# Two attentions with the context on the partitions: maximum and sum by GpSimd, and a written order of the steps

## The chip, the cores and the metric

The kernel runs on one core of a Trainium2 chip. The core has five instruction streams that matter here: TensorE (PE, with its weight loads shown as PEld), VectorE (DVE), ScalarE (ACT), GpSimd (POOL), and SyncE (SP), which in this kernel issues the DMAs. Each engine takes its instructions strictly in its own order and waits where an operand is not ready. The metric is device microseconds of one execution, and less is better.

## The reference

A stack of four layers works on `x` (8 sequences x 112 tokens x 512 channels) with a context of 8 x 375 x 512, all in float32. The first layer is a one-head attention, the second and third are RWKV blocks, the fourth has two 16-head cross attentions and an MLP. The change concerns the two 16-head attentions of the fourth layer:

```python
def _cross_attention(q_in, kv_in, wq, bq, wk, bk, wv, bv, wo, bo, bias_k, bias_v):
    qh = (q_in @ wq + bq).reshape(b, q_len, H, K)          # H = 16 heads of K = 128
    kh = (kv_in @ wk + bk).reshape(b, t, H, K)             # t = 375 context tokens
    vh = (kv_in @ wv + bv).reshape(b, t, H, K)
    kh = concatenate([kh, broadcast_to(bias_k, (b, 1, H, K))], axis=1)   # token 376
    vh = concatenate([vh, broadcast_to(bias_v, (b, 1, H, K))], axis=1)
    logits = einsum('bqhk,bthk->bhqt', qh, kh) / sqrt(K)
    weights = softmax(logits, axis=-1)                     # over the 376 tokens
    ctx = einsum('bhqt,bthk->bqhk', weights, vh).reshape(b, q_len, H * K)
    return ctx @ wo + bo

x = x + _cross_attention(layer_norm1(x), context, ...)
x = x + _cross_attention(layer_norm2(x), context, ...)
x = x + gelu(layer_norm3(x) @ w_fc1 + b_fc1) @ w_fc2 + b_fc2
```

## The kernel before

Everything is held with channels on the 128 partitions: `x` as 4 blocks of 128 channels by 896 tokens (8 batches of 112). The 16 heads are worked in `NG` = 4 groups of `HG` = 4. The value projections of both attentions and part of the first one's keys are made long before, as filler under the RWKV layers, and lie in DRAM (`wvs`, `wks`). The other keys are made inside the attentions, for two batches at a time, by seven block products instead of eight (`chained`, line L1234 for the matmuls, L1237 to L1243 for the copies and adds); one call has 14 pieces. Query and output projections are also seven block products (`seven` and `project7`, L1161; 14 pieces). The sums of weight blocks that these need come from `weight_sums`, four GpSimd operations on 128x512 each (L1135 to L1138), the sums of tokens from `token_sums` on DVE (L1143 to L1146).

For each attention, `attention` loops over the groups, and in each over the 8 batches. For one batch of one group:

- the keys' last column, `bias_k - bk`, is copied by POOL (L1396); the values of the batch are loaded by two DMAs (L1398, L1399) into one buffer;
- for each of the 4 heads one matmul gives the scores, 112 query tokens on the partitions by 376 context tokens (L1403); `softmax` takes the maximum along the free axis on DVE (L232), the exponential with its running sum on ACT (L235), reciprocal and product on DVE (L236, L237); three transposes on TensorE (L1406) turn the result, so that context tokens lie on the partitions;
- the three transposed chunks of 125, 125 and 126 tokens are copied from PSUM (L1410 on ACT, L1412 on DVE), 12 matmuls give the weighted values (L1416), and DVE adds the value bias (L1423).

Then the group's output projection and the next group's queries follow, interleaved. In this stage no order is written out: the framework's scheduler orders the instructions of every engine by its own priorities, and the kernel influences it only through the order in which Python makes them and through the `fill` calls, which put key pieces between the steps of the layer norms. Stages before this one (first layer, RWKV) have `manual_schedule` regions, in which the instructions of PE, DVE, ACT and POOL stand as the program writes them. DMAs on SP are not bound by such a region.

PSUM has eight banks: two for products (`mm`), two for scores, three for transposes, one for weighted values.

Of the kernel before, what the change touches and what calls it, by code (L numbers as in the profile page):

```python
# [29 lines left out]
P = 128  # L30
# [11 lines left out]
HG = 4  # L42
NG = HEADS // HG
T = S + 1
CT = S // 3
# [63 lines left out]
def tile_kernel(ctx: ExitStack, tc: tile.TileContext, d: dict, out: bass.AP):  # L109
# [27 lines left out]
    ones_t, mean_h, less_mean_h = (const.tile([P, P], F32, name=f) for f in ("ones_t", "mean_h", "less_mean_h"))  # L137
    pick = const.tile([P, 4, 4 * HB], F32, name="pick")
# [89 lines left out]

    def softmax(work, scores, n, name):

        top = work.tile([L, 1], F32, tag="top", name=f"top_{name}")
        nc.vector.tensor_reduce(top, scores, AX.X, ALU.max, negate=True)  # L232
        prob = work.tile([L, n], F32, tag="prob", name=f"prob_{name}")
        total = work.tile([L, 1], F32, tag="total", name=f"total_{name}")
        nc.scalar.activation(prob, scores, AF.Exp, bias=top, accum_out=total)  # L235
        nc.vector.reciprocal(total, total)  # L236
        nc.vector.tensor_scalar(prob, prob, total, None, ALU.mult)  # L237
        return prob
# [883 lines left out]
    def weight_sums(pool, tag, w, u):  # L1122


        if tag == "kt":
            y = [pool.tile([P, HG, T], F32, tag=tag, name=f"ws{j}{u}", bufs=4) for j in range(2)]
# [8 lines left out]
        nc.gpsimd.tensor_add(y[0], a21, a22)  # L1135
        nc.gpsimd.tensor_sub(y[1], y[0], a11)
        nc.gpsimd.tensor_sub(y[2], a11, a21)
        nc.gpsimd.tensor_sub(y[3], a12, y[1])  # L1138
# [9 lines left out]
    def seven(ps, work, w, s, b, t, n, put, u):  # L1148
# [25 lines left out]
        for m in range(2):  # L1174
            first.append(bank("k1", m))
            product(first[m], m, lambda k: w[:, k], b11)
            yield
            p1.append(tile_of("rstd", m))
            nc.scalar.copy(p1[m], first[m])
        for m in range(2):  # L1180
            product(first[m], m, lambda k: w[:, 2 + k], b21, start=False)
            yield
            put(0, m, first[m], None)
        for m in range(2):
            p = bank("k6", m)
            product(p, m, lambda k: s()[1][:, k], t[1])
            yield
            u2 = tile_of("u2", m)
            nc.vector.tensor_add(u2, p, p1[m])
            p = bank("k7", m)  # L1190
            product(p, m, lambda k: s()[2][:, k], t[2])
            yield
            u3 = tile_of("u3", m)
            nc.vector.tensor_add(u3, p, u2)
            q = bank("k5", m)
            product(q, m, lambda k: s()[0][:, k], t[0])
            yield
            put(1, 2 + m, q, u3)
# [68 lines left out]
    def attention(i, ident, h_in, work, kv, ps, ps2, keep, near, mlp_norm):  # L1267
# [104 lines left out]
        def some(pieces, n):  # L1372
            for _ in range(n):
                next(pieces)
# [249 lines left out]
```

## Time and profile before

| | us |
|---|---|
| median of 3 runs | 2945.32 (2944.32 to 2945.58) |
| span of the profiled execution, first to last instruction | 2938.3 |
| first key product of the fourth layer starts at | 1414.6 |
| first score matmul of the first 16-head attention at | 1471.9 |
| first score matmul of the second one at | 2126.1 |
| last weighted values end at about | 2742 |

The profiled execution's own time outside its span isn't listed; the median of the runs stands 7.0 us above the span, and this is taken as what lies around it. Times in a profile's row are the mean of one instruction unless said otherwise. An idle time is put beside the instruction that ended it, with what released it. A line of the chain of waits gives start, length and the instruction; a line of the table by stretch gives each engine's busy time in that stretch. TensorE's matmuls overlap, so the distance from one to the next, which the chain shows, is a better price than a row's mean.

### The profile page before, as it was taken

What the parts mean: (1) busy time and instruction counts of PE and PEld (TensorE: products, weight loads), DVE (VectorE), ACT (ScalarE), POOL (GpSimd) and SP (SyncE); (2) the same over time, 40 slices, a digit from 0 to 9 for tenths busy, and PEclk for the clock granted to TensorE, in tenths of its full rate; (3) what the DMA queues carried; (4) which work ended last, traced back from release to release, by engine and by line L of the source; (5) the groups of instructions that cost most, each with busy time, mean ns of one, the idle gap of its engine ahead of it and who ended that gap; (6) DMA issues with size and microseconds to landing.
All of it is one profiled execution on the core that took longest, in us unless ns stands there. A gap on an engine that the chain in (4) does not pass through costs nothing.

```text
span 2938.3 us, 29915 instructions
## 1 busy us (share of the span) xinstructions
PE 2848.3 (97%) x10130; PEld 1555.3 (53%) x10130; DVE 1605.4 (55%) x2408; ACT 1020.6 (35%) x2028; POOL 870.8 (30%) x700
## 2 busy tenths in 40 slices
PE   8989999999999999999899999999999999999999
PEld 4734443344444433356465656566565656656544
DVE  1464288845442788652555555545554554545455
ACT  2232456533243565532331313232331323323311
POOL 1432178744331687641412010100302010000030
PEclk9999999999999999999999999999999999999999
DMA  5721498843311989642243334334332433432110
GB/s 208 231 76 39 156 278 258 265 128 110 99 64 62 281 234 298 184 132 90 101 149 126 124 123 129 109 122 140 102 123 100 133 108 122 139 113 80 47 51 25
DMA packets 198743, 400.82 MB, mean 136 GB/s; under 512 B 33224, under 2 KB 119528, under 8 KB 191808
## 3 DMA queue, kind: packets, MB, share of 16 engines
q1 hardware_dynamic: 198592, 398.91, 43.2%
q8 instruction: 81, 1.33, 0.2%
q14 instruction: 70, 0.57, 0.1%
HBM read 321.06 MB, written 77.91 MB: 136 GB/s over the span
## 4 chain that ended last, share of the span: by engine, by line
PE 83%; DVE 9%; ACT 3%; POOL 3%; issue 2%; DMA 1%; DVEq 0%; POOLq 0%; ACTq 0%; SPq 0%
PE ps_vk L1001 13%; PE ps_k1k L1234 10%; PE ps_k5k L1234 7%; PE av L1416 6%; PE sc L1403 5%; PE ps_o L163 3%; PE pt L1406 3%; PE ps_fk L163 2%; PE ps_k1q L1161 2%; PE ps_r L569 2%; PE ps_k L569 2%; PE ps_k5q L1161 2%; PE ps_fr L163 2%; PE ps_v L569 2%; PE ps_k7q L1161 2%
## 5 line engine op out<-in xcount | busy, mean ns | idle before, releaser
L1001 PE MATMUL ps_vk<-wv,cv 128*128 128x512 f32 x1296 | 581.7, 599 | 13.8 <-ACT k L1099 6.1
L1001 PEld LDWEIGHTS ps_vk<-wv,cv 128*128 128x128 f32 x1296 | 242.8, 191 | 337.3 <-issue 285.0
L1027 POOL TENSOR_TENSOR k<-k,k 128x512 f32<-128x512 f32 (+1 forms) x153 | 197.2, 1289 | 323.4 <-ACT k L1026 276.0
L776 DVE TENSOR_TENSOR_SCAN st<-decay,kv 128x904 f32<-128x904 f32 x128 | 260.7, 2037 | 17.5 <-POOL rs L780 4.8
L780 POOL TENSOR_TENSOR rs<-st,r 128x896 f32<-128x896 f32 x128 | 246.8, 1928 | 51.9 <-DVE st L776 46.8
L235 ACT ACTIVATE prob<-sc,top 112x376 f32<-112x376 f32 x256 | 147.2, 575 | 296.3 <-DVE top L232 168.0
L1396 POOL COPY k<-over_k 128x4 f32<-128x4 f32 x64 | 13.8, 223 | 648.6 <-PE sc L1403 576.6
L1403 PE MATMUL sc<-k,q 128*112 128x376 f32 x512 | 201.2, 485 | 1.6 <-ACT prob L235 1.5
L1416 PEld LDWEIGHTS av<-pts,v 125*128 125x128 f32 (+1 forms) x1536 | 183.4, 191 | 31.0 <-DVE pts L1412 15.8
L1416 PE MATMUL av<-pts,v 125*128 125x112 f32 (+1 forms) x1536 | 187.7, 276 | 1.9 <-DVE pts L1412 0.9
L1234 PE MATMUL ps_k1k<-cs,wsk 128*128 128x375 f32 x480 | 177.8, 478 | 4.6 <-ACT u2k L1237 3.1
L772 DVE TENSOR_TENSOR kv<-vp,k 128x904 f32<-128x904 f32 x128 | 141.5, 1105 | 58.2 <-ACT vp L674 52.4
L232 DVE TENSOR_REDUCE top<-sc 112x1 f32<-112x376 f32 x256 | 139.0, 544 | 53.7 <-PE sc L1403 49.0
L1026 ACT COPY k<-ps_vk 128x512 f32<-128x512 f32 (+1 forms) x153 | 89.1, 582 | 177.0 <-PE ps_vk L1001 174.2
L1099 ACT COPY k<-ps_vk 128x512 f32<-128x512 f32 (+1 forms) x153 | 89.0, 582 | 172.3 <-PE ps_vk L1001 164.2
L1406 PEld LDWEIGHTS pt<-ident_l,prob 112*125 112x125 f32 (+1 forms) x768 | 97.3, 175 | 72.2 <-DVE prob L237 44.8
L1406 PE MATMUL pt<-ident_l,prob 112*125 112x112 f32 (+1 forms) x768 | 120.7, 276 | 2.7 <-DVE prob L237 2.5
L1234 PEld LDWEIGHTS ps_k1k<-cs,wsk 128*128 128x128 f32 x480 | 88.7, 188 | 62.8 <-ACT u2k L1237 4.3
L237 DVE TENSOR_SCALAR prob<-prob,total 112x376 f32<-112x376 f32 x256 | 113.4, 443 | 7.7
L1241 DVE TENSOR_TENSOR k<-ps_k5k,u2k 128x375 f32<-128x375 f32 x52 | 28.5, 549 | 162.2 <-PE ps_k5k L1234 161.2
L674 ACT COPY vp<-vj 128x896 f32<-128x896 f32 x124 | 112.8, 910 | 7.3 <-DMA vj<-rows 3.5
L1423 DVE TENSOR_TENSOR ctxt<-av,bv 128x448 f32<-128x448 f32 x64 | 40.0, 625 | 128.9 <-PE av L1416 128.9
(394 smaller groups left out, 4837.0 us busy)
## 6 DMA issues: line engine op xcount, KB each, us to landing
vj<-rows SPq DMA_DIRECT2D x124, 448.0 KB
cv<-blocks SPq DMA_DIRECT2D x181, 251.5 KB
cs<-blocks SPq DMA_DIRECT2D x120, 375.0 KB
wvs<-k SPq DMA_DIRECT2D x128, 256.0 KB
v<-wvs SPq DMA_DIRECT2D x64, 512.0 KB
cx<-in_ctxT SPq DMA_DIRECT2D x38, 750.0 KB
v<-wvs SPq DMA_DIRECT2D x64, 252.0 KB
wvs<-k SPq DMA_DIRECT2D x64, 224.0 KB
```

Of the source, the lines that this page charges most:

```text
L163: nc.tensor.matmul(p, w[:, k, o * P : (o + 1) * P], rhs(k, h), start=k == 0, stop=k == NC - 1)
L235: nc.scalar.activation(prob, scores, AF.Exp, bias=top, accum_out=total)
L569: nc.tensor.matmul(y, ws[f][:, c, o * P : (o + 1) * P], x_f, start=c == 0, stop=c == NC - 1)
L776: nc.vector.tensor_tensor_scan(flat(st), flat(decay[:, c]), flat(kv), 0.0, ALU.mult, ALU.add)
L780: nc.gpsimd.tensor_mul(by_batch(rs), st[:, :, :L], by_batch(r[:, c, :]))
L1001: nc.tensor.matmul(to, left, right, start=start and n == 0, stop=k == 1, skip_group_check=True)
L1027: nc.gpsimd.tensor_add(y, z, y)
L1161: nc.tensor.matmul(to, lhsT, rhs, start=start and k == 0, stop=k == 1, skip_group_check=not start)
L1234: nc.tensor.matmul(y, lhsT, rhs, start=start and k == 0, stop=k == 1, skip_group_check=True)
L1403: nc.tensor.matmul(sc, q[:, o, tok], kt[:, o, :], start=True, stop=True)
L1406: nc.tensor.transpose(pt[t][:nt, o, :], prob[:, t0 : t0 + nt], ident[:L, :L])
L1416: nc.tensor.matmul(av[:, o, :], v[:nt, t, o * HD : (o + 1) * HD], pts[:nt, t, o, :], start=t == 0, stop=t == 2,)
```

## The change

In the 16-head attentions, the scores are computed the other way round: keys are the stationary operand in three chunks of 128 context tokens (the chunks overlap by three; the keys' tiles have two more columns, `TK` = 378, for the last one), and the result has context tokens on the partitions and query tokens along the free axis. The transposes and their copies go away. The work is cut into units of two heads of one batch, 16 a group, 128 in all. For one unit (lines of the new file):

- `scores`: 6 matmuls of 112 columns (L1424); ACT copies the first chunk and DVE takes the maximum with the other two (L1432, L1434); GpSimd takes the maximum across the partitions and writes it to all of them (L1436, a `partition_all_reduce` of 128x224);
- `exponentials`: DVE subtracts the maximum from the three chunks, 672 columns (L1442); ACT takes the exponentials of 448 and 224 columns, with a bias of -1e30 on the rows that a chunk has too many (L1444);
- `chunk_sums`: two DVE adds of 224 columns (L1449, L1450); `total`: GpSimd sums across the partitions (L1454); `inverse`: DVE reciprocal of 128x224 (L1458);
- `weighted`: 6 matmuls (L1465) on the unnormalized exponentials; `finish`: DVE multiplies by the reciprocal (L1478), ACT adds the value bias (L1480).

The whole loop stands in a `manual_schedule` region. In step k the program writes: load of the values for unit k+1, sum across partitions of unit k-1, scores and maximum of unit k, reciprocal of k-1, a key piece, exponentials of k, a key piece, weighted values and finish of k-1, chunk sums of k, further key pieces. A count spreads the pieces of the next two batches' keys over four steps; where few are left, the last four steps take pieces of the output projection instead.

GpSimd does no additions in this stage any more: the weight sums, and the adds of `chained` outside the first norm, go to DVE. Values are loaded by half batches into three buffers. In `seven` and `chained` the evacuation of a product now stands before the generator's `yield` and not after it. PSUM has three banks for products, four for scores (two tiles of two), one for weighted values. Two constant tiles of the RWKV layers are freed before the fourth layer. The built program has two POOL instructions more that change the engine's loaded code, one ahead of the first maximum, one ahead of the MLP's weight sums.

```diff
-                for o in range(HG):
-                    sc = ps2.tile([L, T], F32, tag="sc", name=f"sc{u}_{o}", bufs=2)
-                    nc.tensor.matmul(sc, q[:, o, tok], kt[:, o, :], start=True, stop=True)
-                    prob = softmax(work, sc, T, f"{u}_{o}")
-                    for t, (t0, nt) in enumerate(CHUNKS):
-                        nc.tensor.transpose(pt[t][:nt, o, :], prob[:, t0 : t0 + nt], ident[:L, :L])
...
-                for t, (_, nt) in enumerate(CHUNKS):
-                    if t == 1:
-                        nc.scalar.copy(pts[:nt, t], pt[t][:nt])
-                    else:
-                        nc.vector.tensor_copy(pts[:nt, t], pt[t][:nt])
...
+        def scores(gr, k, q):
...
+            sc = ps2.tile([P, 4, 256], F32, tag="sc", name=f"sc{u}", bufs=2)
+            for t in range(3):
+                for y in range(2):
+                    o = 2 * half + y
+                    nc.tensor.matmul(
+                        sc[:, t, y * L : (y + 1) * L],
+                        kt[:, o, t * CT : t * CT + P],
+                        q[:, o, b * L : (b + 1) * L],
+                        start=True,
+                        stop=True,
+                    )
+            top = work.tile([P, n], F32, tag="top", name=f"top{u}", bufs=2)
+            nc.scalar.copy(top, sc[:, 0, :n])
+            for t in (1, 2):
+                nc.vector.tensor_max(top, sc[:, t, :n], top)
+            tops = work.tile([P, n], F32, tag="tops", name=f"tops{u}", bufs=1)
+            nc.gpsimd.partition_all_reduce(tops, top, P, ReduceOp.max)
+            return [u, gr, k, sc, top, tops]
+
+        def exponentials(it):
+            u, gr, k, sc, top, tops = it
+            pts = work.tile([P, 3, n], F32, tag="pts", name=f"pts{u}", bufs=2)
+            nc.vector.tensor_sub(pts, sc[:, :3, :n], tops.unsqueeze(1).to_broadcast([P, 3, n]))
+            for t, y in ((slice(2), 0), (slice(2, 3), 1)):
+                nc.scalar.activation(pts[:, t], pts[:, t], AF.Exp, bias=rests[:, y : y + 1])
+            it[3] = pts
+
+        def chunk_sums(it):
+            u, gr, k, pts, top, tops = it
+            nc.vector.tensor_add(top, pts[:, 0], pts[:, 1])
+            nc.vector.tensor_add(top, pts[:, 2], top)
+
+        def total(it):
+            each = work.tile([P, n], F32, tag="each", name=f"each{it[0]}", bufs=1)
+            nc.gpsimd.partition_all_reduce(each, it[4], P, ReduceOp.add)
+            it[5] = each
+
+        def inverse(it):
+            nc.vector.reciprocal(it[5], it[5])
...
+        with tc.manual_schedule(engines=ORDERED):
+            for gr in range(NG):
...
+                for k in range(2 * B):
+                    key = (i, gr, 2 * (k // 4) + 2) if k < 12 else (*following, 0) if following else None
+                    left = ready[key] - shared["emitted"] if key else 0
+                    if k == 12:
+                        early = left < 8 or following != (i, gr + 1)
+                        w_q = query_weight(gr + 1) if gr + 1 < NG else None
+                    count = left if early else -(-left // (4 - k % 4))
...
+                    if k + 1 < 2 * B:
+                        vs[k + 1] = load_values(gr, k + 1)
+                    if before:
+                        total(before)
+                    it = scores(gr, k, q)
+                    if before:
+                        inverse(before)
+                    take(more_keys(key, int(count > 1)))
+                    exponentials(it)
+                    take(more_keys(key, 1))
+                    if before:
+                        weighted(before, vs.pop(k - 1))
+                        finish(before, ctxt, t_c)
+                    chunk_sums(it)
+                    take(more_keys(key, count - 1 - int(count > 1)))
+                    if k == 1 and not ends:
+                        s_o = weight_sums(keep, "ws", w_o, f"o{i}_{gr}", nc.vector)
+                    if k >= 12 and early:
+                        take(out_pieces, 1)
+                    before = it
...
-            tc.tile_pool(name="t3p", bufs=2, space=PSUM) as ps,
+            tc.tile_pool(name="t3p", bufs=3, space=PSUM) as ps,
```

## The prediction

> **What bounds the kernel now.** I read the page's busy shares first, then the same shares by stretch, then the chain that ended last inside one head group, and last the groups with their durations. The page, engines with share of the span:
>
> ```profile
> PE 2848.3 (97%) x10130; PEld 1555.3 (53%) x10130; DVE 1605.4 (55%) x2408; ACT 1020.6 (35%) x2028; POOL 870.8 (30%) x700
> PEclk9999999999999999999999999999999999999999
> ```
>
> TensorE is busy 97% at an ungated clock; but a share is no limit, so the stretch of one head group (stretch, its length, busy time of PE, PEld, DVE, ACT, POOL, clock, DMA share, GB/s):
>
> ```profile
> 1872.00:2040.00 168.00, 167.66 (x691) 105.27 (x690) 84.27 (x191) 47.24 (x123) 17.14 (x20) 1.00 0.38 121
> ```
>
> PE has no hole in it, DVE is half idle, POOL nine tenths idle: in the attentions the time is PE's instructions, and these can be priced by the chain (start, length, what, records):
>
> ```profile
> 1913.78 1.26 PE ps_k5k L1234 x4
> 1930.20 1.26 PE sc L1403 x4
> 1933.35 0.66 PE pt L1406 x6
> 1939.18 2.67 PE av L1416 x24
> ```
>
> An f32 matmul is two records, a transpose one. So a score matmul of 376 columns costs 0.63 us, a transpose 0.11, a matmul of 112 columns 0.222, a key product of 375 columns 0.63.
>
> **Part 1: what leaves PE.** Removed are 256 score matmuls x 0.632 = 162 us and 768 transposes x 0.110 = 84 us; added 768 score matmuls of 112 columns (6 per unit of two heads of one batch, 128 units) x 0.222 = 171 us, by the row of `av`, which has that shape. The 768 matmuls of `av` stay. Net: 75 us less PE work. From the first key product at 1414.6 to the end, all PE work priced this way is 1467 of 1524 us; I take the other 57 us (norms, the MLP's starts) as unchanged. If PE stays the only limit, the span goes from 2938.3 to 2863.
>
> **Part 2: what the units now wait for.** The unit's chain in the new order is: POOL maximum (L1436), DVE subtraction from PSUM (L1442), ACT exponentials of 448 and 224 columns (L1444), DVE adds of the three chunks (L1449, L1450), POOL sum (L1454). On POOL's queue the sum of unit k stands ahead of the maximum of unit k+1, so the units do not overlap on this chain: it is a loop, and one turn is the shortest possible step. Rows for its links (line, engine, form, count, then busy, mean ns of one, idle before):
>
> ```profile
> L1423 DVE TENSOR_TENSOR ctxt<-av,bv 128x448 f32<-128x448 f32 x64 | 40.0, 625 | 128.9 <-PE av L1416 128.9
> L1241 DVE TENSOR_TENSOR k<-ps_k5k,u2k 128x375 f32<-128x375 f32 x52 | 28.5, 549 | 162.2 <-PE ps_k5k L1234 161.2
> L591 ACT ACTIVATE decay<-e 128x448 f32<-128x448 f32 x16 | 9.0, 576 | 0.3
> L1237 ACT COPY u2k<-ps_k1k 128x375 f32<-128x375 f32 x60 | 28.2, 471 | 47.7 <-PE ps_k1k L1234 47.7
> L1144 DVE TENSOR_TENSOR t_c<-ctxt,t_c 128x224 f32<-128x224 f32 x28 | 10.9, 389 | 0.5
> L706 DVE RECIPROCAL gsq<-gsq 128x224 f32<-128x224 f32 x32 | 48.2, 1523 | 24.7 <-ACT gsq L701 24.7
> ```
>
> Subtraction, 672 columns: DVE's PSUM rows rise 76 ns over 73 columns, so 625 + 224 x 1.04 = 0.86 us. Exponential of 448: 0.58; of 224: 0.58 less 224 x 0.84 ns (ACT's 375 and 448 column copies, 471 and 532 ns) = 0.39. The first add runs beside the second exponential; the second add is 0.39. Four hand-overs between engines, 0.04 to 0.1 each in the instructions by time, 0.3. Together 2.5 us, so a turn is P = 2T + 2.5, where T is one POOL reduction of 128x224. A second floor: between the sum of unit k-1 and the subtraction of unit k DVE has a reciprocal (1.52, L706) and, in most steps, a key add (0.55), so P is at least T + 2.1 + 2.5. Behind the waiting subtraction DVE holds the product, the chunk adds and the next key adds, and PE waits for the key adds to give its product banks back; so PE can't run far ahead of a late reduction.
>
> **T is not in this trace.** POOL's nearest rows:
>
> ```profile
> L1396 POOL COPY k<-over_k 128x4 f32<-128x4 f32 x64 | 13.8, 223 | 648.6 <-PE sc L1403 576.6 <-PE ps_fr L163 43.9 <-DVE over_k L1323 28.0
> L971 POOL COPY wv<-wx 128x1024 f32<-128x1024 f32 x1 | 1.2, 1206 | 1.2 <-PE ps_vk L1001 1.2
> L547 POOL TENSOR_TENSOR v<-v,xa 128x448 f32<-128x448 f32 x16 | 18.1, 1130 | 5.8 <-DVE v L544 5.8
> ```
>
> From below: it must read and write 224 columns once, 0.22 + 224 x 0.96 ns (the two copies) = 0.44 us. From above: joining 128 rows by pairs is seven two-operand passes; the two-operand row gives 2.52 ns a column, 0.565 a pass, 4.0 us. It combines values rather than moves them, so it is nearer the two-operand row than the copy, and some of the seven levels will run inside one pass: I take 2.5 us, between four and five passes. This is the weakest number here and both ends stay in the range.
>
> The Trainium skill speaks against the change. "GPSIMD Engine Reference", section 3.2, gives 247,699 ns for a reduction along partitions at [128, 2048]; that is another instruction, and no run here shows it. An estimate from that figure is 121 ns a column, 27 us for 224 columns, and with 256 of them the span would grow by over 6 ms.
>
> **Part 3: turn against PE's step.** The new program's lists say what PE has in each of the 128 steps (12 matmuls of 112 columns, 2.66 us, plus key products or projection pieces): 44 steps of 7.7 us, 44 of 6.5, 4 of 6.4, 3 of 5.7, 7 of 5.2, 9 of 4.2, 6 of 3.9, 2 of 2.7, one of 19; the last step of each of the 8 groups has 50 us or more of projections and keys behind it and covers any turn taken here. The key products are spread over a group's first 12 or all 16 steps; groups whose keys come from DRAM, and the second attention's first, leave steps thin. A step costs the larger of P and its PE work. At T = 2.5, P = 7.5, the excess is 44 x 1.04 + 4 x 1.1 + 3 x 1.8 + 7 x 2.3 + 9 x 3.3 + 6 x 3.6 + 2 x 4.8 = 133 us. Sum: -75 + 133 = +58.
>
> **Part 4: costed at nothing, with the cover.** DVE takes over the weight sums (12 of 128x512 a group; between the DVE rows of 0.39 for 224 and 1.09 for 896 columns about 0.69 each, 8 us a group). With two maxima, reciprocal, subtraction, product, two adds (4.3 us), key adds (0.8), token sums (0.4) and these sums it has about 6.0 us a step. That lies under 7.1, the mean of a full PE step, and under P; if that cover goes, DVE at 6.0 would itself be the step of the thin ones. ACT has about 3 us. POOL loses its additions in this stage. Values are loaded by half a batch, 256 DMA issues where 128 were, 0.33 us each on SP's queue: 43 us over 1.3 ms, each load a step ahead with three buffers, and one landing in the chain took 3.6 us; if SP came late, up to that much per step. A POOL code change stands before the first reduction and one before the MLP's sums; in this trace such a configuration at 0.9 us took 11 ns, and the first lies under the query products (56 records x 0.376 = 21 us). "GPSIMD Engine Reference", section 2.1, puts a first call to new code at about 6 us, which that cover would also hide. PSUM for products goes from two banks to three; the MLP's idle PE, 9 us in its last 196, bounds that gain. The late half of the last group's output product still ends behind its norm, as before; I take no change.
>
> Span 2938.3 + 58 = 2996; the runs' median of 2945.3 stands 7.0 above the span, so 3003.
>
> **Rivals.**
> A. The loop fits under PE and the kernel is faster. It decides at P = 6.75, T = 2.1, where the excess equals 75 us. At T = 1.7 the second floor rules, P = 6.3, excess 50: 2920. At T = 0.44, P = 5.0, excess 19: 2889. For it: POOL is nine tenths idle and two short operations per step fit. Against: T would have to be under four two-operand passes.
> B. T is at or beyond the upper end. At 4.0 P is 10.5, excess 480: 3350; POOL is then the bound outright. For it: seven levels of joining. Against: seven full passes over memory is the slowest way that the rows suggest.
> C. T is small enough but DVE's order bites: with reciprocal, key adds that wait for PE and weight sums in one queue, a full step becomes 7.6 instead of 7.1. 88 full steps x 0.5 us = 44 on top of about 50: excess 94, 2964. For it: DVE at 6.0 of 7.1 us, in order, and its two-operand rows grow where POOL works beside them (L547 on DVE: 0.99 us for 448 columns, against 0.62 elsewhere). Against: PE may run a step ahead, two score tiles exist.
>
> **How the numbers follow.** Forecast (T between 2.2 and 4, time 2955 to 3350) 0.42; A 0.34; break-even, T about 2.05 to 2.15, 0.06; B 0.10; C 0.08. Faster by over 0.2% (what a measurement can tell) 0.34, within 0.06, slower 0.60. The range runs from A's end, 2889, to a little past T = 4, 3380; left out are most of B and little else. Alone, the forecast's own range is 2955 to 3350.
>
> **What would show it.** In the profile after: the all-reduces' mean duration on L1436 and L1454 against 2.1 us; in a middle group, idle time of PE at L1465 or L1424 released by ACT or DVE (forecast) or none (A); POOL idle before L1454 ended by DVE and before L1436 by nothing, if the loop rules; DVE idle before L1442 ended by POOL. PE busy in the attentions should fall by 75 us in every case. Wrong would make it: T off, or a scheduler's order on SP that delays the values.

## The result, and where the time went

| | before | after |
|---|---|---|
| median of the runs, us | 2945.45 (2944.32 to 2947.14) | 3046.84 (3043.49 to 3049.44) |
| ratio | 1 | 1.0349, 95% interval 1.0334 to 1.0363 |
| span of the profiled execution, us | 2938.3 | 3044.9 |
| attention stage, us | 1472.0 to 2742.0: 1270.0 | 1472.7 to 2848.8: 1376.1 |
| PE busy in it, us, and mean granted clock | 1255.7 at 1.00 | 1235.9 at 0.96 |
| PE idle in it, us | 14.3 | 140.2 |
| from its end to the span's end, us | 196.3 | 196.1 |

The stage begins with the first score matmul of the first 16-head attention. Before, it is taken to end with the last weighted values; after, with the first matmul of the MLP's norm. What PE has left behind these two points differs by four matmul records, 1.5 us. The change makes the kernel 3.5% slower, 101 us; the forecast was plus 58. All of it lies in this stage: plus 106.1 of plus 106.6 us of span. The sign was right and the time lies inside the range, but the reasons that were given are not the ones that hold.

First the page of the kernel after: busy time and share of the span by engine, the granted clock by slice, then four groups of instructions (line, engine, operation, tiles, count, then busy time and mean ns of one, then the idle time of the engine ahead of them and what ended it).

```profile
PE 2833.0 (93%) x10386; PEld 1601.2 (53%) x10386; DVE 1789.0 (59%) x2457; ACT 1056.8 (35%) x2081; POOL 1065.7 (35%) x851
...
PEclk9999999999999999999999999998999999999999
...
L1454 POOL PARTITION_ALL_REDUCE each<-top x128 | 209.6, 1638 | 461.9 <-DVE top L1450 461.9
L1436 POOL PARTITION_ALL_REDUCE tops<-top x128 | 126.5, 988 | 585.8 <-DVE top L1434 585.8
...
L1424 PE MATMUL sc<-q,k 128*128 128x112 f32 x1536 | 212.9, 283 | 98.0 <-POOL k L1417 97.1
...
L1458 DVE RECIPROCAL each<-each 128x224 f32<-128x224 f32 x128 | 197.8, 1545 | 26.1 <-POOL each L1454 26.1
```

Two things stand in these lines. The reductions that the prediction took as 2.5 us each last 0.99 us (maximum) and 1.64 us (sum), and POOL is idle ahead of most of them (all 128 sums and 105 of the 128 maxima): POOL does not set the pace by being busy. And PE, idle for 14 us in the whole stage before, now waits 97.1 us ahead of its score matmuls for one instruction that the prediction mentions only as a yardstick: POOL's copy of the keys' last columns (L1417), 0.31 us long.

The answer on waits, for PE's longest (engine, line, what it waited for: us in total, times, longest):

```profile
PE sc L1424 <- POOL k L1417: 97.1, 55, 6.0
PE ps_k5k L1228 <- DVE wsk L1129: 13.3, 5, 5.8
PE ps_k6q L1155 <- DVE ws1q L1130: 12.2, 6, 2.0
```

Why so short an instruction is waited for shows in the instructions by time (start, length, engine, line, operation, records; in brackets the idle time before and what ended it), in a thin stretch of the second head group:

```profile
1668.40 1.44 PE L1228 MATMUL ps_k1k<-cs,w_L_xattn_wk 128*128 128x375 f32 x4
...
1671.00 1.06 PE L1424 MATMUL sc<-q,k 128*128 128x112 f32 x8
...
1674.23 1.61 POOL L1454 PARTITION_ALL_REDUCE each<-top  x1 [3.12 <-DVE top L1450]
...
1675.72 0.26 POOL L1417 COPY k<-over_k 128x12 f32<-128x12 f32 x1
1676.03 0.93 PEld L1424 LDWEIGHTS sc<-q,k 128*128 128x128 f32 x4 [4.15 <-POOL k L1417]
1676.03 1.19 PE L1424 MATMUL sc<-q,k 128*128 128x112 f32 x4 [3.97 <-POOL k L1417]
...
1677.02 2.73 PE L1228 MATMUL ps_k1k<-cx,w_L_xattn_wk 128*128 128x375 f32 x4
```

PE has done four of the six score matmuls of an even unit at 1672. The last two need the third chunk of the keys, with the columns 375 to 377 that POOL writes. In the written order that copy stands in `scores(k)`, and `total(k-1)` stands ahead of it on POOL's queue. So it can't start before the sum of the unit before, the sum not before the chunk adds on DVE, and these not before ACT's exponentials. PE therefore waits, at nearly every even unit (55 of 64), for a part of the chain of the unit before, and where the step is thin for most of it. The copy was on POOL before the change too, but there no reduction stood ahead of it on the queue.

The last line holds the second cost. Two key products of the same shape, four records, take 1.44 us at 1668 and 2.73 us right after the wait. The table by stretch (stretch, length, then busy time of PE, PEld, DVE, ACT, POOL, granted clock, DMA share, GB/s) first gives the whole stage of the kernel before, then that of the kernel after and two stretches around the wait:

```profile
1472.00:2742.00 1270.00, 1255.73 (x5242) 790.49 (x5240) 675.45 (x1479) 377.26 (x938) 144.64 (x164) 1.00 0.37 120
...
1472.72:2848.80 1376.08, 1235.90 (x5506) 834.64 (x5504) 852.10 (x1514) 407.66 (x985) 345.86 (x321) 0.96 0.36 110
1672.00:1676.00 4.00, 0.06 (x1) 0.00 (x0) 1.53 (x4) 1.96 (x5) 1.75 (x2) 0.86 0.51 156
1678.00:1679.00 1.00, 1.00 (x3) 0.42 (x3) 0.97 (x3) 0.00 (x0) 0.32 (x1) 0.50 0.00 0
```

After the idle time the clock is 0.50, and between 1681 and 1682 it comes back. This splits the 106 us, if PE's work falls by the predicted 75, to 1255.7 - 75 = 1181 us at full clock: measured busy time is 1235.9, so the lower clock costs about 55 by this estimate; idle time grows by 140.2 - 14.3 = 126. The sum is -75 + 55 + 126 = +106. (The granted clock, laid over PE's busy time in the trace, gives 48 us lost; the work then fell by 68.) "TensorE: Matmul & The Clock Gate" of the Trainium skill, Part 1, "What's actually happening", says that the array runs at half clock after an idle window of about 3.4 us and at full clock again after about 3.4 us of work; the 0.50 and the slowed matmuls from 1677 to 1682 agree with the two states. Where the rule falls short is told at the end.

### The profile page after: what moved, and what is told of

It reads as the page before. It is cut to its first block, busy times and chain, and to the rows that moved or that the text cites. A ratio compares the mean times of both kernels' runs of the same rounds, so it can differ in the third digit from the quotient of the medians.

```text
span 3044.9 us, 31264 instructions
## 1 busy us (share of the span) xinstructions
PE 2833.0 (93%) x10386; PEld 1601.2 (53%) x10386; DVE 1789.0 (59%) x2457; ACT 1056.8 (35%) x2081; POOL 1065.7 (35%) x851
## 4 chain that ended last, share of the span: by engine, by line
PE 64%; DVE 18%; POOL 7%; ACT 5%; issue 3%; DMA 2%; SPq 0%; DVEq 0%; ACTq 0%; POOLq 0%
PE ps_vk L994 13%; PE ps_k5k L1228 5%; PE ps_k1k L1228 4%; POOL each L1454 4%; DVE each L1458 4%; PE sc L1424 4%; PE ps_o L167 3%; PE av L1465 2%; DVE pts L1442 2%; ACT pts L1444 2%; DVE top L1434 2%; PE ps_k1q L1155 2%; PE ps_fk L167 2%; PE ps_r L562 2%; PE ps_k L562 2%
## 5 line engine op out<-in xcount | busy, mean ns | idle before, releaser
L1454 POOL PARTITION_ALL_REDUCE each<-top x128 | 209.6, 1638 | 461.9 <-DVE top L1450 461.9
L1436 POOL PARTITION_ALL_REDUCE tops<-top x128 | 126.5, 988 | 585.8 <-DVE top L1434 585.8
L1424 PE MATMUL sc<-q,k 128*128 128x112 f32 x1536 | 212.9, 283 | 98.0 <-POOL k L1417 97.1
L1424 PEld LDWEIGHTS sc<-q,k 128*128 128x128 f32 x1536 | 200.9, 196 | 142.6 <-POOL k L1417 107.2
L1444 ACT ACTIVATE pts<-pts,rests 128x448 f32<-128x448 f32 (+1 forms) x256 | 133.2, 567 | 311.2 <-DVE pts L1442 311.2
L1434 DVE TENSOR_TENSOR top<-sc,top 128x224 f32<-128x224 f32 x256 | 100.1, 391 | 212.5 <-ACT top L1432 207.9
L1465 PEld LDWEIGHTS av<-pts,v 125*128 125x128 f32 (+1 forms) x1536 | 202.0, 202 | 32.5 <-issue 5.1
L1458 DVE RECIPROCAL each<-each 128x224 f32<-128x224 f32 x128 | 197.8, 1545 | 26.1 <-POOL each L1454 26.1
L1465 PE MATMUL av<-pts,v 125*128 125x112 f32 (+1 forms) x1536 | 202.7, 284 | 1.6 <-issue 1.3
L1432 ACT COPY top<-sc 128x224 f32<-128x224 f32 x128 | 44.3, 346 | 405.3 <-PE sc L1424 405.3
L1442 DVE TENSOR_TENSOR pts<-sc,tops 128x672 f32<-128x672 f32 x128 | 105.1, 821 | 9.3 <-POOL tops L1436 9.3
```

Of the source, the lines that this page charges most:

```text
L1424: nc.tensor.matmul(sc[:, t, y * L : (y + 1) * L], kt[:, o, t * CT : t * CT + P], q[:, o, b * L : (b + 1) * L], start=True, stop=True,)
L1434: nc.vector.tensor_max(top, sc[:, t, :n], top)
L1442: nc.vector.tensor_sub(pts, sc[:, :3, :n], tops.unsqueeze(1).to_broadcast([P, 3, n]))
L1444: nc.scalar.activation(pts[:, t], pts[:, t], AF.Exp, bias=rests[:, y : y + 1])
L1454: nc.gpsimd.partition_all_reduce(each, it[4], P, ReduceOp.add)
L1458: nc.vector.reciprocal(it[5], it[5])
```

## The experiments

Three theories were set against each other. Theory 1: the wait for the copy, and the clock after it, made the kernel slow. Theory 2, the prediction's: the two reductions in series on POOL set the step. Theory 3, the prediction's rival C: DVE's order sets it, the reciprocal above all. Each ratio is to the kernel before on the same chip; two chips were used, and a difference between two runs is that of their medians, which the ratios put up to 5 us higher or lower. The table has every run, with PE's busy and idle time between the first score matmul and the MLP's norm.

| run | time, us | ratio, 95% interval | stage | PE busy | PE idle | clock |
|---|---|---|---|---|---|---|
| changed kernel | 3046.8 | 1.0349 (1.0334 to 1.0363) | 1376.1 | 1235.9 | 140.2 | 0.96 |
| copy ahead | 2958.9 | 1.0045 (1.0030 to 1.0060) | 1294.3 | 1207.5 | 86.8 | 0.98 |
| reciprocal late | 3108.3 | 1.0544 (1.0520 to 1.0567) | 1441.3 | 1258.8 | 182.5 | 0.94 |
| maximum ahead of sum | 3021.3 | 1.0259 (1.0237 to 1.0281) | 1355.0 | 1218.9 | 136.0 | 0.97 |
| useless work in the waits | 3034.1 | 1.0297 (1.0280 to 1.0315) | 1363.5 | 1247.4 | 116.1 | 0.98 |
| copy ahead, reciprocal late | 2979.6 | 1.0124 (1.0107 to 1.0140) | 1306.2 | 1207.7 | 98.4 | 0.98 |
| copy ahead, maximum twice | 3020.9 | 1.0271 (1.0252 to 1.0290) | 1354.9 | 1225.7 | 129.2 | 0.97 |
| copy ahead, sums on POOL | 3106.8 | 1.0556 (1.0540 to 1.0572) | 1439.1 | 1220.2 | 218.9 | 0.93 |
| copy ahead, one maximum | 2958.6 | 1.0049 (1.0032 to 1.0067) | 1288.3 | 1203.7 | 84.6 | 0.98 |
| copy and some sums ahead | 2933.9 | 0.9960 (0.9946 to 0.9974) | 1261.6 | 1195.5 | 66.1 | 0.99 |
| copy and all sums ahead | 2922.5 | 0.9930 (0.9916 to 0.9944) | 1254.9 | 1195.0 | 59.9 | 0.99 |
| the same, one maximum | 2917.7 | 0.9913 (0.9899 to 0.9927) | 1245.8 | 1193.6 | 52.3 | 0.98 |

### The copy alone moved

```diff
 def scores(gr, k, q):
-    if not half:
-        nc.gpsimd.tensor_copy(kt[:, :, S:], ...)
+    last_keys(gr, b)              # only where not yet done
...
     nc.gpsimd.partition_all_reduce(tops, top, P, ReduceOp.max)
+    if half:
+        last_keys(*((gr, b + 1) if b + 1 < B else (gr + 1, 0)))   # the same copy, for the next batch
```

> Edit: POOL's copy of the keys' last columns for the next batch is issued right behind the maximum of the odd unit, one step earlier than in the changed kernel, so that it no longer stands behind that unit's sum; nothing else is moved. Theory 1 (the wait that the prediction missed): PE's wait for this copy ahead of the fifth score matmul, 97 us in 55 places of the changed kernel's profile, and the lower clock after the long ones among them are what made the kernel slow; both go, and the time is 2890 to 2940 us, about 2915, which is what the prediction's own rule gives for reductions of 0.98 and 1.63 us. Theory 2 (the prediction's loop): the sum standing ahead of the next maximum on POOL sets the step; the copy is only where the wait shows, PE's idle time moves from the score matmuls to the products of the values and the key products, and the time stays within 25 us of 3047. Theory 3 (DVE's order): the reciprocal and the subtraction behind it set the step; 3020 or more.

Measured: 2958.9 us, 88 us less, from 0.3 us of work that was put ahead of one instruction instead of behind it. PE's idle time falls by 53 us, its busy time by 28 with the clock. The same answer on PE's waits now, for this kernel, begins with other lines:

```profile
PE av L1475 <- ACT pts L1454: 18.0, 12, 4.8
PE ps_k5k L1228 <- DVE wsk L1129: 15.9, 5, 6.2
PE ps_k5k L1228 <- ACT k L1230: 12.3, 8, 2.5
PE ps_k6q L1155 <- DVE ws1q L1130: 12.2, 6, 2.0
```

The wait for the copy is down to 5.2 us in 4 places. The sum still stands ahead of the next maximum, so theory 2 (within 25 us of 3047) falls. Theory 1 holds for most of the loss, but not for all: 2959 is above its range of 2890 to 2940, and PE's idle time is still 72 us above that of the kernel before.

### The reciprocal behind the subtraction

```diff
 it = scores(gr, k, q)
-if before:
-    inverse(before)
 take(more_keys(key, int(count > 1)))
 exponentials(it)
+if before:
+    inverse(before)
```

> Edit: DVE's reciprocal of unit k-1 goes from ahead of the subtraction of unit k to behind it; the copy stays where it is in the changed kernel. Theory 1 (POOL's copy behind the sum): the subtraction comes 0.3 to 1.5 us earlier, but the reciprocal then stands ahead of the chunk adds, so that the sum and the copy behind it come at most 1 us earlier; 3047 less 0 to 60 us. Theory 2 (reductions in series on POOL): no change, within 15 us. Theory 3 (DVE's order is the step): the 1.5 us reciprocal leaves the loop in each of 128 steps; 2900 to 2950.

Measured: 3108.3 us, 61 us slower than the changed kernel. Theory 3 in its form with the reciprocal falls. Theory 1 had the sign wrong: the reciprocal (1.55 us) ran beside POOL's maximum (0.99 us) before, so that the subtraction gains little by its absence, and behind the subtraction it lasts longer than the exponentials (1.04 us by time) and holds up the chunk adds. The sum comes later and with it the copy. The waits of this kernel say so, PE's first and then one of DVE's (the subtraction now waits for the maximum, 9.3 us in the changed kernel):

```profile
PE sc L1424 <- POOL k L1417: 127.1, 56, 6.6
...
DVE pts L1442 <- POOL tops L1436: 102.3, 84, 2.0
```

### Maximum ahead of the sum

```diff
-if before:
-    total(before)
 it = scores(gr, k, q)
+if before:
+    total(before)
 take(more_keys(key, int(count > 1)))
 exponentials(it)
+if before:
+    inverse(before)
```

> Edit: on POOL the copy and the maximum of unit k go ahead of the sum of unit k-1, and on DVE the reciprocal of k-1 goes behind the subtraction of k. This opens the prediction's loop and takes the copy from behind the sum at once. Theory 1: as fast as the run with the copy alone moved, 2890 to 2940, since only the copy mattered. Theory 2: clearly faster than the run with the copy alone moved, 2890 to 2930 against about 3047. If the later sum makes the product and so the one bank of weighted values late, slower than the copy alone by up to 1 us in each of the 128 steps.

Measured: 3021.3 us, 62 us above the copy alone. PE no longer waits for the copy (5.0 us in 5 places), but opening the prediction's loop in this way brings nothing. POOL now waits for the maximum's input in all units but one, and the sum stands behind it: DVE's reciprocal waits for the sum in 124 units, 97.4 us, where that was 31 units and 26.1 us in the changed kernel. That the product and the bank of weighted values then come late in their turn is argued; the waits show PE held up for the product by 5.7 us only. One line of this kernel's waits on POOL:

```profile
POOL tops L1436 <- DVE top L1434: 982.6, 127, 75.3
```

The edit moves the reciprocal too. The run with the copy ahead and the reciprocal late, below, has that without the turned order, at 2979.6 us; the turned order by itself thus costs some 42 of the 62 us. An order of two instructions on one queue can be wrong either way; what mattered most was which of them stood in front of the third, the copy.

### Useless work in the waits

```diff
+late = {(1, 0): (2, 4, 14), (1, 1): (2, 4, 14), (1, 2): (2, 4), (1, 3): (14,), (2, 0): (2, 4)}
 for t in range(3):
+    if t == 2 and k in late.get((i, gr), ()):
+        for _ in range(8):
+            nc.tensor.matmul(sc[:, 3, :n], kt[:, 2 * half, :P], q[:, 2 * half, :n], start=True, stop=True)
```

> Edit: the changed kernel with work added: at 11 places where PE waited 3.1 to 6.0 us for POOL's copy (54 us together), PE gets 8 useless matmuls of 224 columns (about 0.4 us each, 3.2 us, into an unused quarter of the scores' tile) ahead of the waiting matmul. If the lower clock after a long idle time is a cost by itself (the two key products after a wait of 3.97 us took 2.73 and 2.50 us in place of 1.44, at a granted clock of 0.50), the added work is hidden by the waits and the time falls by 15 to 30 us, to 3017 to 3032. If the idle time alone costs, the time is unchanged, 3047 to 3052.

Measured: 3034.1 us, 13 us less with 35 us more work (88 matmuls at 3.21 us for eight); the intervals of the two ratios do not overlap. The table by stretch around two of the long waits, first for this kernel:

```profile
1656.00:1684.00 28.00, 24.99 (x142) 20.23 (x141) 19.16 (x34) 9.68 (x25) 10.41 (x9) 1.00 0.39 123
```

and for the changed kernel, with the same columns:

```profile
1656.00:1684.00 28.00, 19.40 (x91) 14.44 (x90) 18.10 (x31) 8.93 (x22) 8.79 (x8) 0.82 0.36 110
```

With the array kept busy the clock stays at 1.00 where it was 0.82, and 142 matmul records fit where 91 did (32 of the 142 are the useless ones). So the low clock is a cost apart from the idle time. The gain is a little under the 15 to 30 us expected (by the ratios it is 15).

### Copy ahead and reciprocal late

> Edit: the copy moved as in the first run, and DVE's reciprocal of k-1 behind the subtraction of k. With the copy alone moved the time was 2959 us; the reciprocal alone moved made the changed kernel slower by 61 us. Theory 1a (the reciprocal's delay hurt there only through the sum and the copy behind it): with the copy out of the way the sum's end releases no score matmul, the subtraction comes up to 1.5 us earlier, and the time is 2930 to 2959. Theory 3 (DVE's order sets the thin steps): the loop from sum over reciprocal, subtraction, exponentials and adds to the next sum is 5.9 us, and with the reciprocal beside the exponentials 5.2 us; faster by 10 to 30 us. Against both: the reciprocal now holds up the product that gives back the one bank of weighted values; then 2960 to 3000.

The edit is the first two together. Measured: 2979.6 us, 20.7 us slower than the copy alone. The copy is out of the sum's way here, so the reciprocal's place hurts by itself, as the last of the three expectations had it. The two profiled executions differ by 12 us (that of the copy alone, with a span of 2964.0, was the longest of its six), and all of it is idle time of PE, among it 7.2 us of waits for the product on DVE, which gives the bank of weighted values back (the longest 5.8 us); the run with the copy alone lists none.

### The maximum twice

```diff
-nc.gpsimd.partition_all_reduce(tops, top, P, ReduceOp.max)
+for _ in range(2):
+    nc.gpsimd.partition_all_reduce(tops, top, P, ReduceOp.max)
```

> Edit: the copy moved as in the first run, and each maximum across the partitions is done twice into the same tile, so that the unit's chain on POOL grows by 0.98 us in each of 128 units. The prediction's loop with the measured durations is 0.98 + 1.63 + 2.5 = 5.1 us and its second floor over the reciprocal 1.63 + 4.6 = 6.2 us; the doubled maximum makes the loop 6.1, still under the second floor and under the 6.5 and 7.7 us of PE work of 88 steps: 2959 plus 0 to 25 us. If the whole chain from the score matmuls on is in series in the thin steps (some 36 of 128), plus 35 us; if in all steps, plus 125 us, 3085.

Measured: 3020.9 us, 62 us above the copy alone: 42 us of idle time and 18 us of clock. The page's row confirms the added time per unit:

```profile
L1445 POOL PARTITION_ALL_REDUCE tops<-top x256 | 252.2, 985 | 511.1 <-DVE top L1442 496.7
```

42 us at 0.98 us is 43 units of 128. The two traces show which steps grew. From one unit's first score matmul to the next, the 27 steps with less than 6.2 us of PE work took 18 us more than with the copy alone, the 48 of 6.4 or 6.5 us 14 us more, the 44 of 7.7 us 18 us more, and the ends of the groups 9. So the length of a reduction is not hidden in the full steps either. The time lies between the second of the three expectations and the third. The rule of two floors, by which the maximum would hardly matter, is refuted.

### The weight sums back on POOL

```diff
-s_o = weight_sums(keep, "ws", w_o, f"o{i}_{gr}", nc.vector)
+s_o = weight_sums(keep, "ws", w_o, f"o{i}_{gr}", nc.gpsimd)
```

and likewise for the sums of keys and queries.

> Edit: the copy moved as in the first run, and the weight sums of the two attentions (four operations on 128x512, three times a group) back on POOL, where they were before; POOL's code is then changed some 40 times more. If these changes are as short as the two in the changed kernel's profile (11 ns each), POOL has 5.2 us (4 of 1.29 us, by the kernel's other sums on it) between two reductions three times a group, and PE's waits for the sums on DVE (28 us with the copy moved) go or become waits for POOL: 2940 to 2990. If a change of code costs microseconds, it shows as idle time of POOL ahead of the first operation after it: at 6 us each 40 of them are 240 us of POOL's time, of which the thin steps would pass on at least half, 3050 or more.

Measured: 3106.8 us, 148 us above the copy alone. The prediction had called a change of POOL's code 11 ns by a row of the kernel before. In the instructions by time of this kernel, POOL alone:

```profile
1571.12 1.02 POOL L1444 PARTITION_ALL_REDUCE tops<-top  x1
1581.29 1.25 POOL L1129 TENSOR_TENSOR wsk<-w_L_xattn_wk 128x512 f32<-128x512 f32 x1 [9.15 <-issue]
...
1585.06 1.26 POOL L1132 TENSOR_TENSOR wsk<-w_L_xattn_wk,wsk 128x512 f32<-128x512 f32 x1
1592.38 1.63 POOL L1464 PARTITION_ALL_REDUCE each<-top  x1 [6.05 <-issue]
```

Between operations of different code POOL stands still for 6 to 9 us with nothing that the profile shows to wait for: 60.2 us in 10 places ahead of sums across the partitions, 53.9 in 7 ahead of the keys' sums. "GPSIMD Engine Reference" of the Trainium skill, section 2.1, puts the first call of new code at about 6 us without an instruction in the profile; the 6.05 agrees. The configuration rows, 4 to 15 ns ahead of a reduction and 81 to 88 ns ahead of the sums (11 and 88 in the changed kernel), do not hold that time. With 129 us of such idle time in 19 places and the sums' own 5 us each time in POOL's queue, this is the dearest of the edits: keeping the weight sums off GpSimd inside the loop is worth 148 us, and the prediction saw only the cost on DVE. How the 148 us divide between the changes of code and the place of the sums in the queue was not separated.

### One reduction for the maximum over the chunks

```diff
-nc.scalar.copy(top, sc[:, 0, :n])
-for t in (1, 2):
-    nc.vector.tensor_max(top, sc[:, t, :n], top)
+nc.vector.tensor_reduce(top, sc[:, :3, :n].rearrange("p t n -> p n t"), AX.X, ALU.max)
```

> Edit: the copy moved as in the first run, and the maximum over the three chunks taken by one DVE reduction over 3 x 224 columns from PSUM in place of ACT's copy and two DVE maxima. By the subtraction's row (672 columns, 0.82 us) it should take about 0.82 us, against 0.35 + 0.3 + 0.82 of the three: the chain from the scores to the maximum is 0.5 to 0.6 us shorter, ACT loses 0.35 us a unit. If the chain from the scores on matters in the thin steps, 10 to 25 us faster than 2959; if not, the same within 8 us. If the strided reduction is slow (over 1.5 us), slower than 2959.

Measured: 2958.6 us against 2958.9: no difference. The strided reduction is as fast as the subtraction's row suggested:

```profile
L1440 DVE TENSOR_REDUCE top<-sc 128x224 f32<-128x672 f32 x128 | 109.4, 855 | 101.0 <-PE sc L1432 101.0
```

So the step is shorter at its beginning: from the last score matmul's end to the start of the maximum it takes 1.06 us in the median, where it took 1.46 with the copy alone. That is 0.4 us, not the 0.5 to 0.6 expected, and the time doesn't follow. This limits what the doubled maximum showed: not every link of the chain counts by its length. Which wait takes over stays open.

### The weight sums moved, not removed

```diff
+if k == 11 and following and ("wk", *following, 0) not in shared:
+    begin_sums(following)        # two of the keys' four sums; the others at the second key piece
...
-if k == 1 and not ends:
-    s_o = weight_sums(keep, "ws", w_o, f"o{i}_{gr}", nc.vector)
+if 4 <= k < 8 and not ends:      # one of the four sums a step
+    add_of(s_o[k - 4], y, z)
...
 if gr + 1 < NG:
+    first_sums()                 # two of the queries' four, into free value tiles
     take(pieces, 4)
```

> Edit: the copy moved as in the first run, and DVE's weight sums moved off the places where PE waited for them: the first two sums for the queries' projection go into two free value tiles and are made ahead of the output projection's last pieces; two of the four sums for the next group's keys are made at the end of step 11 (or, where the first keys come from DRAM, at the group's end) instead of between reciprocal and subtraction of step 12; the four sums for the output weights are spread over steps 4 to 7 instead of all in step 1. No operation is added or taken away. With the copy alone moved (2959 us) PE waited 12.2 us for the queries' sums and 15.9 us for the keys' sums, and these waits of 2 to 6 us lowered the clock after them. If those waits and their clock are what is left, the time falls by 20 to 40 us, to 2920 to 2940, under the 2945 us of the kernel before. If DVE's order only moves the wait to the next place (the adds that give the product banks back), 2950 to 2960.

Measured: 2933.9 us, 25 us less and under the kernel before. The queries' sums are gone from PE's waits; of the keys' sums two waits stayed, 14.3 us, at the ends of the two groups whose next keys come from DRAM, and one of 1.4 us.

```diff
-if k == 11 and following and ("wk", *following, 0) not in shared:
+if k == 11 and following:
     begin_sums(following)
+if k == 14 and following in begun and early:
+    begun[following][2]()        # the other two
```

> Edit: as the run before (2934 us), but the sums for the next group's keys are begun at the end of step 11 in every group and finished by step 14 in the three groups whose next first keys come from DRAM or whose next group is the other attention's. There PE still waited 7.84, 6.50 and 1.39 us for them. If these waits go and nothing takes their place: 14 to 25 us faster, 2910 to 2920. If the two sums at the end of step 11 or 14 make the maxima behind them late in these thin steps, 3 groups x 1.4 to 2.8 us come back, 2918 to 2928.

Measured: 2922.5 us, 11 us less: under the 14 to 25 expected if nothing took their place, inside the 6 to 16 expected if the sums make the maxima behind them late. That it was those maxima is argued, not shown.

> Edit: as the third variant of the sums, and the maximum over the chunks by one DVE reduction instead of ACT's copy and two maxima, and one key piece more in step 0 of a group and one less in step 1. ACT loses 44 us; PE waited 14.9 us for ACT's copies of key products and 13.7 us for ACT's exponentials. If ACT's order is what makes those late, up to 10 us faster than the run without these two edits; otherwise within 6 us, as the single reduction made no difference (2959 against 2959) when only the copy was moved.

Measured: 2917.7 us, ratio 0.9913 (0.9899 to 0.9927), the fastest kernel of this study and 0.9% under the one before. The two last edits bring 4.8 us, within the 6 us of the second expectation; the intervals overlap, so they are not shown to matter. Its page gives these busy times:

```profile
PE 2790.3 (96%) x10386; PEld 1578.2 (54%) x10386; DVE 1799.6 (62%) x2329; ACT 1012.7 (35%) x1953; POOL 1068.8 (37%) x851
```

and the answer on PE's waits begins, inside the stage, with

```profile
PE ps_k5k L1228 <- ACT k L1230: 12.3, 11, 2.6
PE av L1513 <- ACT pts L1492: 12.2, 9, 2.8
PE ps_k1k L1228 <- ACT p1k L1230: 10.8, 3, 4.1
```

PE's busy time over the whole span is 58 us less than before the change, 2790.3 against 2848.3, with some low clock still in it, and what PE waits for now is ACT's order. Of the waits for the sums none is left; for the copy PE still waits 7.3 us in 6 places.

## Why the prediction was right in sign and wrong in its reasons

That the time came out slower, as forecast, was luck: by the forecast's own rule the measured reductions were short enough for a faster kernel, and two costs that its sum did not hold made it slower.

- **Part 1, 75 us less PE work: right.** The busy time of the best kernel's stage is 1193.6 us, 62 under the 1255.7 of before, at a clock of 0.98; the mean clock over the stage leaves at most 24 us of slowing in it, so the work fell by 62 to 86. The prices hold too: 12 records of `av` start 1.33 us apart from the next, which is six matmuls at 0.222. The sentence that PE's busy time should fall by 75 us "in every case" was wrong: in the attentions it fell by 20, from 1255.7 to 1235.9, because the clock did not stay at 1.00. The prediction priced no clock at all.
- **Part 2, T = 2.5 us: the mis-sized term.** Measured are 0.99 and 1.64 us, inside the bounds of 0.44 and 4.0, and nearer to the copy's rows than to seven two-operand passes. Both are under the break-even of 2.1. By the prediction's own rule, with these values, the loop is 0.99 + 1.64 + 2.5 = 5.1 us and the second floor 1.64 + 4.6 = 6.2; the histogram's steps under 6.2 then lack 48 us, and the time would be 3003 - 133 + 48 = 2918. So the forecast's case fell with T, and rival A should have come.
- **Part 2, POOL's queue: the step that failed.** It named what stands ahead of the maximum on that queue and left out what else stands there: the copy, whose row (L1396 before) it quoted as a price only. The wait was not the maximum's, it was PE's own score matmul, two instructions further. Moving the copy gave 88 us back; that much is shown. The order on POOL that was named, sum ahead of maximum, is not what cost: turned round, it was slower than left as it was, by some 42 us beside the run with the copy ahead and the reciprocal late.
- **Parts 2 and 3, a step as the larger of turn and PE work: wrong in form.** Twice the maximum cost 62 us where the rule said nearly nothing, a shorter path to the maximum gave nothing, and the reciprocal taken out of the loop made it slower. The turn is not the shortest possible step either: with 5.1 us for the loop and 6.2 for the second floor, some of the 27 thin steps lasted 3.87 us, in the changed kernel as in the best one, just their PE work. A thin step by itself can thus cost nothing. In the best kernel the 27 took 146 us, 26 more than the PE work in them, where the rule gives 48 more; and the 44 full steps took 28 us more than their work, where it gives none.
- **Part 4, weight sums on DVE at nothing: wrong.** The cover was DVE's mean load, 6.0 us of 7.1; the loss came from their place in the queue, 25 us of PE waits in the changed kernel. Moving them without removing any gave 25 and then 11 us. That is what rival C said in general, DVE's order rather than its load. Its price of 44 us is near the 36 by luck: it put 0.5 us on each of 88 full steps, and the waits of the changed kernel stood in 11 places, at the sums.
- **Part 4, POOL's code: the row misread, the conclusion right.** The 11 ns is not the price; 6 to 9 us is. In the changed kernel the two changes lie where POOL waits anyway, as the prediction said: the first reduction waits for DVE, and the MLP's sums for a DMA (55.6 us). The loads of the values did no harm either: no wait of PE for a DMA is listed in the stage.
- **The Trainium skill's estimate of 27 us a reduction** from "GPSIMD Engine Reference", section 3.2, does not carry over: the all-reduce took 0.99 and 1.64 us for 128x224. The prediction was right not to use it.
- **The signs that it named.** "POOL idle before L1436 by nothing" was wrong (585.8 us, for DVE), and so was idle time of PE at L1424 released by ACT or DVE (it was POOL). POOL's idle time before L1454, ended by DVE, came as said (461.9 us). Read as written, the two misses refute the forecast's mechanism, though the time came out on its side.

So the kernel was slower for reasons outside the prediction's sum: 88 us for the copy's place and the clock after its waits, and 36 us for the place of the sums. With both moved, the change is 0.7% faster than before, and 0.9% with the single maximum, at the 2918 us that rival A's rule gives with the measured reductions. That the total then agrees is luck and no proof of that rule, which the doubled maximum and the lengths of the steps refute. What the third bank for products and the earlier evacuation of a product contribute was not measured apart.

## What to carry to other kernels

When an order is written out by hand, list for every queue each short instruction that stands behind a long chain, and ask who waits for it: a 0.3 us copy behind a sum cost 88 us here. A wait of TensorE of a few microseconds can be dearer than its length, because the matmuls after it may run at half clock; here filler work gave back the clock, and moving the cause both. And a mean load that fits under the step says nothing about a burst of four operations in the middle of one engine's order.

## What the hardware showed beyond expectation

- On GpSimd the sum across 128 partitions of 224 float32 columns takes 1.64 us and the maximum 0.99 us, the same shape and the same kind of instruction.
- A change of GpSimd's code stood as 6 to 9 us of idle time that no instruction shows (60.2 us in 10 places, 53.9 in 7), beside configuration rows of 4 to 88 ns.
- The clock fell to 0.50 after waits shorter than a window of 3.4 us. In the run with the copy alone moved, PE waited 2.04 us for the queries' sums six times; after two of these the next four records of 448 columns took 3.35 and 2.79 us in place of 1.77, and the other four waits left the clock at 1.00. The trace shows what sets the two apart. In it the clock changes on a grid of 3.41 us (it fell at 1667.09 and 1946.98, 82 such pieces apart, and rose one piece later each time). Laid along this grid, the wait that ends at 1946.99 lies in one piece, but for 0.01 us; the one that ends at 1620.57 is shared by two:

```profile
1943.57:1946.98 3.41, 1.38 (x4) 0.38 (x2) 3.03 (x6) 0.00 (x0) 0.00 (x0) 1.00 0.70 252
1946.98:1950.39 3.41, 3.40 (x5) 1.76 (x6) 1.16 (x2) 0.00 (x0) 0.00 (x0) 0.50 0.14 55
...
1615.89:1619.30 3.41, 2.64 (x8) 0.99 (x6) 2.84 (x6) 0.00 (x0) 0.00 (x0) 1.00 0.35 96
1619.30:1622.71 3.41, 2.14 (x6) 1.21 (x7) 2.65 (x5) 0.00 (x0) 0.00 (x0) 1.00 0.51 211
1622.71:1626.10 3.39, 3.39 (x11) 1.72 (x10) 1.67 (x3) 0.00 (x0) 0.00 (x0) 1.00 0.00 0
```

The second of the two waits that lowered the clock lies whole in a piece too, with PE busy 1.37 us of it; the other three that did not are shared by two pieces, with PE busy 2.04 us or more in each. In this run's stage 13 of 363 pieces at 1.00 were followed by one at 0.50, and PE was busy 1.53 us or less in each of the 13; of the 350 others one had 1.49 us and the rest 1.71 or more. So in this trace it is not the length of a wait that decides, but how much of one piece it leaves idle. "TensorE: Matmul & The Clock Gate", section "Why this matters for your kernels", advises against gaps above some 3 us; by these rows that is not a safe limit.
